# A message-passing layer on one core: the tasks beside its batches dealt anew, early products kept in DRAM, a fifth buffer of gathered rows

## The chip, the cores and the metric

The kernel runs on one core of a Trainium2 chip. The metric is the device time of one execution in microseconds (us). The core's engines run side by side, each through its own queue in order: TensorE (PE, with its weight loads PEld) multiplies matrices, VectorE (DVE) and ScalarE (ACT) work on elements, GpSimd (POOL) issues the gathers, SyncE (SP) issues other transfers. They wait for one another by semaphores.

## The reference

1250 nodes have 512 features each, 384 as 128 vectors of three and 128 scalars s. 40000 edges are sorted by their target `dst`. Two rounds of messages follow each other; cut to what matters:

```python
x_j = x[src]
s_j = silu(x_j[:, 384:] @ W1 + b1) @ W3 + b3
split = s_j * (rbf * cutoff @ W2 + b2)             # rbf, cutoff: functions of edge_weight
s1, s2, s3 = thirds of split
v_msg = v_j * s1[:, :, None] + s3[:, :, None] * edge_attr[:, None, :]
x = x + segment_sum([v_msg, s2], dst)              # first round
x_j = x[src]
... v @ U, (v @ U) @ V, norm, an MLP with Wu1, Wu2: a row of 512 for each edge
x = x + segment_sum(msg, dst)                      # second round
out = layernorm(x_in + x)
```

A row of the second round depends on the source node alone. So it is computed once for each node, and its sum over edges is a product of a 1250 x 1250 table of edge counts with the table of rows.

## The kernel before

**Head.** For each of ten blocks of 128 nodes, `table_row` makes a row of 640 for every node, and SP writes it to a table in DRAM. Between these rows stand transposings of the edges' data (`beside`).

**Batches.** The edges are cut into 20 groups of 16 tiles of 128 edges, and a batch `t` is four tiles (80 batches, the last four smaller). `gather(t)` has POOL fetch 4 x 128 rows of the table by four indirect transfers into a buffer `rows_t` (four buffers, `ROWS`). `edge_factors(t)` has PE make the factors `eb` in four PSUM banks, of which there is one set. `messages(t)` has DVE multiply rows by factors (two instructions, L799 and L802, with `make_pair`, L816, between them). `add_messages(t)` has PE sum the messages by target node with one-hot matrices (`hot`, `spread`) into `agg`. ACT's `mark_sources` and DVE's `make_pair` make matrices whose product, `count_links`, counts edges for each pair of source and target in `adj`. `close_group` has ACT copy `agg` and split the counts (`high`, `both`); DVE's `add_counts` brings them into the table of counts.

**Tasks beside the batches.** A step of the main loop emits gather(t+2), messages(t), the list `first`, add_messages(t-1) and count_links(t-1), the list `early`, edge_factors(t+1), the list `late` and the list `dve`. The lists, by step, are written out by hand; they set the order of each engine's queue. In them stand the making of the next group's basis, `hot` and `spread` (`make_turns`, `make_basis`, `turn_basis`, `make_hot`, `make_spread`), and for each block of nodes whose two groups are closed a chain from `sum_block` over `take_block`, `turn_nodes`, `times_u`, `times_uv`, `lengths`, `root`, `hidden`, `curve`, `factors`, `scale_row` and `end_row` to `part_row`, which leaves a block of the second round's rows as three bf16 parts. All of these use one PSUM bank, `work`, in turn, and ACT or DVE must copy out what PE put there before PE can use it again.

**Units.** The output block b needs, for each source block a, a unit of three matmuls (counts by the three parts). Units whose rows are ready are begun in the loop (`begin_out`): 37 of 100, for seven output blocks. Six sums are copied to SBUF tiles of their own (`begun_b`, 2048 bytes a partition each), the seventh stays in PSUM.

**Tail.** `load_x` and `load_rest` bring x and x1 (`resid`, kept in DRAM) back, POOL adds them and the begun sums, PE does the remaining 63 units between the links of the last block's chain and behind it, `end_out` and `norm_out` add, normalize and write each block.

Of the kernel before, what the change touches and what calls it, by code (L numbers as in the profile page):

```python
# [20 lines left out]
P = 128  # L21
# [14 lines left out]
CPG = 4  # L36
# [501 lines left out]
def windowed(tc, sh):  # L538
# [20 lines left out]
    ROWS = 4  # L559
# [34 lines left out]
    resid = tc.dram_tile([NP, width], F32, name="resid")  # L594
    counts = sh.counts
# [10 lines left out]
    with tc.tile_pool(name="msg", bufs=4) as pool, tc.tile_pool(  # L606
# [15 lines left out]
        quarter = pool.tile([P, 1], F32, name="quarter", bufs=1)  # L622
        fade = pool.tile([P, NE], F32, name="fade", bufs=1)
# [8 lines left out]
        def ratios():  # L632
            nc.vector.tensor_scalar(ratio, every, 1.0 / R_CUT, 1.0, op0=ALU.mult, op1=ALU.min)
            nc.vector.memset(quarter, 0.25 * TWO_PI)

# [66 lines left out]
        def make_turns(g, n, part):  # L702
# [16 lines left out]
            if part == 3 or part == 2 and g > 0:  # L719
                nc.scalar.activation(args, args, AF.Sin, scale=TWO_PI)  # L720
# [44 lines left out]

        def mark_sources(t):

            g, i = batches[t]
            one = pool.tile([P, CPG, P], F16, name="one", bufs=3)
            for j in tiles(g, i):  # L770
                e = g * EPG + i * CPG + j
                nc.scalar.activation(one[:, j, :], number[:, :P], AF.Abs, bias=low[:, e : e + 1])  # L772
            for j in tiles(g, i):
                e = g * EPG + i * CPG + j
                nc.scalar.activation(  # L775
                    one[:, j, :], one[:, j, :], AF.Relu,
                    scale=less[:, e : e + 1], bias=worth[:, e : e + 1],
                )
            onehots[t] = one
# [13 lines left out]
        def messages(t):  # L793
# [6 lines left out]
            make_pair(t)  # L800
            for js, n, m in runs(g, i):
# [64 lines left out]
        def close_group(g):  # L866
# [5 lines left out]
            else:  # L872
                if g + 2 < NGR:
                    assert rows == P
                    sums[g + 2] = pool.tile([P, width], F32, name="sums_1", bufs=2)
                    nc.scalar.copy(sums[g + 2][P - WIN :, :], agg[P - WIN :, :])
# [3 lines left out]
                rows = min(rows, KEPT)  # L880
                nc.scalar.copy(sums[g][:rows, :], agg[:rows, :])
# [7 lines left out]
            boths[g] = both  # L889

        def add_counts(g):
            both = boths.pop(g)
# [3 lines left out]
            del adjs[g]  # L896

# [19 lines left out]
        def sum_block(b):  # L917
            blk = work()
            for k in range(2):
                nc.tensor.matmul(  # L920
                    blk, sh.sel[:, k, :], sums.pop(2 * b + k), start=(k == 0), stop=(k == 1)
                )
            blks[b] = blk
# [152 lines left out]
        def load_x(first):  # L1076
# [5 lines left out]
            for b in range(first, first + n):  # L1082
                if b in (0, NB - 1):
                    load_nodes(nc.scalar, sh, to, b, b + 1, cols, first)
            inner = [b for b in range(first, first + n) if b not in (0, NB - 1)]
            load_nodes(nc.scalar, sh, to, inner[0], inner[-1] + 1, cols, first)
            for k in range(n):
                kept[first + k] = to[:, k, :]

        def load_rest(first):  # L1090
            n = min(5, NB - first)
            to = five_rows("msg", 2)
            nc.scalar.dma_start(to[:, :n, :], rows_from(resid, first, n))
# [20 lines left out]
        def begin_out(b, a, last, kept):  # L1114
            if a == 0:
                accs[b] = ps_sum.tile([P, BANK], F32, name="begun")
            products(accs[b], b, a, a + 1, a == 0, last and not kept)
# [12 lines left out]
        def end_out(b):  # L1130
# [8 lines left out]
            nc.vector.tensor_scalar(scale[:, 0:1], moments[:, 1:2], EPS, None, op0=ALU.add)  # L1139
            nc.scalar.activation(scale[:, 0:1], scale[:, 0:1], AF.Sqrt)  # L1140
            ending[b] = row, moments, scale

        def norm_out(b):
            row, moments, scale = ending.pop(b)
            nc.vector.reciprocal(scale[:, 0:1], scale[:, 0:1])
            nc.vector.tensor_scalar(
                scale[:, 1:2], moments[:, 0:1], scale[:, 0:1], -1.0, op0=ALU.mult, op1=ALU.mult
            )
# [13 lines left out]
        def at(when, step, fn, *args):  # L1162
            when.setdefault(step, []).append((fn, args))

        def pair_turns(g, part, t):
            n = min(2, NGR - g)
            if n > 0:
                at(dve, t, make_turns, g, n, part)

        for k in range(3):  # L1170
            pair_turns(1, k, 0)
        for g in range(NGR):
            at(early, last_step[g] + 1, close_group, g)
            at(dve, last_step[g] + 1, add_counts, g)
        for t, (g, i) in enumerate(batches):
            if t + 1 < NT:
                at(early, t, mark_sources, t + 1)
            if g + 1 < NGR:
                if g % 2:
                    if i == 0:  # L1180
                        at(dve, t, make_hot, g + 1)
                        at(early, t, turn_basis, g + 1)
                    elif i == 1:
                        at(dve, t, make_spread, g + 1, 0)
                        pair_turns(g + 2, 0, t)
                    elif i == 2:
                        at(dve, t, make_spread, g + 1, 1)
                else:
                    if i == 1:
                        at(dve, t, make_hot, g + 1)  # L1190
                    elif i == 2:
# [504 lines left out]
```

## Time and profile before

| | us |
|---|---|
| median of 10 runs (546.73 to 554.81) | 551.78 |
| the profiled execution | 546.12 |
| its span, first to last instruction | 544.3 |
| first gather starts | 34.12 |
| last multiply of batch 75 ends | 461.69 |
| last multiply of batch 79 ends | 481.00 |
| PE's last matmul ends | 535.37 |

The page gives busy time of each engine, the chain that ended last, and groups of instructions with mean time and with what ended the idle time in front of them. "Issue" is a gap for which the profile shows no other cause. A row of the timeline is a start, a duration, the engine, the line, output and inputs, and in brackets the idle time before it and who ended that.

### The profile page before, as it was taken

How to read it: one execution, taken by the hardware profiler on the slowest of the kernel's cores; microseconds unless marked ns; L12 is line 12 of the kernel's file. 1: busy time of each engine (PE TensorE's matmuls, PEld its weight loads, DVE VectorE, ACT ScalarE, POOL GpSimd, SP SyncE). 2: the span in 40 equal slices, each digit the busy share in tenths (PEclk: the TensorE clock that was granted, in tenths of full speed). 3: DMA queues.
4: the chain of work that ended last, by engine and by line, in shares of the span. 5: the costliest groups of instructions: out<-in, count | busy, mean ns of one | idle time of the engine just before them, and what ended most of it. 6: DMA issues, size and time to landing. Idle time of an engine off the chain costs nothing.

```text
span 544.3 us, 11102 instructions
## 1 busy us (share of the span) xinstructions
PE 439.8 (81%) x4280; PEld 235.0 (43%) x4318; DVE 429.3 (79%) x594; ACT 359.3 (66%) x897; POOL 362.1 (67%) x364
## 2 busy tenths in 40 slices
PE   3946777878878778888987888887989788999993
PEld 2522333444444344444444444544545444445441
DVE  6687988888978998697897899789789689550681
ACT  1436476695795885779579588687867958723342
POOL 7337777777777777777777777677777774100960
PEclk9976878989889988897998999999899899999998
DMA  8658888888878878888787887778787876109131
GB/s 249 212 181 240 251 250 260 258 256 257 264 234 249 267 236 248 262 253 249 245 262 229 252 259 230 233 236 252 233 247 240 250 225 187 49 5 346 50 136 61
DMA packets 35178, 121.18 MB, mean 223 GB/s; under 512 B 6365, under 2 KB 7912, under 8 KB 35116
## 3 DMA queue, kind: packets, MB, share of 16 engines
q0 software_dynamic: 26016, 104.86, 62.9%
q1 hardware_dynamic: 5124, 9.69, 4.9%
q10 hardware_dynamic: 3976, 5.82, 3.1%
q8 instruction: 36, 0.59, 0.4%
q14 instruction: 26, 0.21, 0.1%
HBM read 111.89 MB, written 8.46 MB: 221 GB/s over the span
## 4 chain that ended last, share of the span: by engine, by line
PE 30%; DVE 27%; DMA 18%; POOL 8%; issue 7%; ACT 7%; DVEq 0%; POOLq 0%; ACTq 0%
DMA rows_t<-table,src_i 12%; DVE msg L802 11%; POOL rows_t L691 7%; DVE msg L799 5%; PE agg L833 5%; PE eb L787 5%; DMA wu_sb<-in_L_gnn_Wu_dram 4%; PE agg L840 4%; PE work L981 3%; DVE pair L816 3%; PE adj L1105 2%; PE agg L1105 2%; PE eb L1105 2%; ACT one L775 2%; DVE spread L760 1%
## 5 line engine op out<-in xcount | busy, mean ns | idle before, releaser
L691 POOL DMA_INDIRECT rows_t<-table,src_i x313 | 325.6, 1040 | 118.8 <-issue 79.6
L802 DVE TENSOR_TENSOR msg<-rows_t,eb 128x1536 f32<-128x1536 f32 (+1 forms) x81 | 137.0, 1692 | 0.0
L775 ACT ACTIVATE one<-one,weight,src_f 128x128 f16<-128x128 f16 x313 | 128.1, 480 | 0.2 <-DVE magic L674 0.2
L799 DVE TENSOR_TENSOR msg<-rows_t,eb 128x1024 f32<-128x1024 f32 (+1 forms) x81 | 95.4, 1179 | 38.2 <-PE eb L787 29.3
L787 PE MATMUL eb<-w_sb,basis_t 21*128 21x384 f32 x626 | 77.1, 548 | 57.5 <-DVE msg L802 56.3
L772 ACT ACTIVATE one<-number,low 128x128 f16<-128x128 f16 x313 | 99.4, 389 | 2.5 <-DVE low L665 1.4
L833 PE MATMUL agg<-msg,hot 128*32 128x512 f32 x626 | 96.4, 673 | 0.0
L840 PEld LDWEIGHTS agg<-msg,spread 128*32 128x32 f32 x1878 | 62.5, 121 | 58.0 <-issue 57.5
L840 PE MATMUL agg<-msg,spread 128*32 128x128 f32 x1878 | 76.7, 296 | 0.0
L787 PEld LDWEIGHTS eb<-w_sb,basis_t 21*128 21x128 f32 x626 | 27.1, 187 | 82.3 <-issue 51.5
L1105 PEld LDWEIGHTS <-counts 128*128 128x128 f16 x300 | 29.1, 99 | 27.6 <-issue 2.5
L1098 POOL TENSOR_TENSOR msg<-msg,rows_t 128x512 f32<-128x512 f32 (+1 forms) x10 | 13.7, 1379 | 37.5 <-PE eb L1105 37.5
L816 DVE TENSOR_TENSOR pair<-number,column 128x640 f16<-128x640 f16 (+1 forms) x81 | 38.4, 475 | 0.0
L760 DVE TENSOR_TENSOR spread<-hot,attr 128x768 f32<-128x768 f32 x40 | 37.9, 949 | 0.0
L858 PE MATMUL adj<-pair,one 128*128 128x160 f16 x313 | 37.7, 245 | 0.0
L893 DVE SCALAR_TENSOR_TENSOR both<-both,adj 128x400 f16<-128x400 f16 (+1 forms) x20 | 11.3, 567 | 31.6 <-ACT both L888 29.1
L981 PE MATMUL work<-ident,square 128*128 128x128 f32 x60 | 14.0, 379 | 20.7 <-ACT basis_t L743 20.6
L1038 ACT COPY x<-work 128x128 f32<-128x128 f32 x10 | 2.7, 266 | 41.2 <-PE work L981 41.2
L858 PEld LDWEIGHTS <-one 128*128 128x128 f16 x313 | 21.1, 101 | 18.0 <-issue 15.2
L833 PEld LDWEIGHTS agg<-msg,hot 128*32 128x32 f32 x626 | 13.1, 111 | 33.4 <-issue 25.1
L1105 PE MATMUL begun<-store,counts 128*128 128x512 bf16 x84 | 25.1, 379 | 1.7
L743 ACT COPY basis_t<-work 128x512 f32<-128x512 f32 x20 | 11.5, 576 | 22.7 <-PE work L738 22.7
(170 smaller groups left out, 560.6 us busy)
## 6 DMA issues: line engine op xcount, KB each, us to landing
rows_t<-table,src_i POOLq DMA_INDIRECT x313, 4.1
resid<-x SPq DMA_DIRECT2D x10, 256.0 KB
msg<-resid ACTq DMA_DIRECT2D x2, 1280.0 KB
rows_t<-in_x_dram ACTq DMA_DIRECT2D x2, 1024.0 KB
out_dram<-msg SPq DMA_DIRECT2D x8, 256.0 KB
table<-msg SPq DMA_DIRECT2D x6, 320.0 KB
store<-in_x_dram POOLq DMA_DIRECT2D x2, 768.0 KB
table<-rows_t SPq DMA_DIRECT2D x4, 320.0 KB
```

The costliest lines, as they stand in the source:

```text
L691: nc.gpsimd.indirect_dma_start(out=rows_t[:n, j, :], out_offset=None, in_=sh.table1, in_offset=bass.IndirectOffsetOnAxis(ap=sh.src_i[:n, g ...
L760: nc.vector.tensor_mul(spread[g][:, at], hots[g][:, at, None, :].to_broadcast([P, n, 3, WIN]), sh.attr[:, g, at, :, None].to_broadcast([P, ...
L772: nc.scalar.activation(one[:, j, :], number[:, :P], AF.Abs, bias=low[:, e : e + 1])
L775: nc.scalar.activation(one[:, j, :], one[:, j, :], AF.Relu, scale=less[:, e : e + 1], bias=worth[:, e : e + 1],)
L787: nc.tensor.matmul(eb[:, j, :V], turned[g][rows, i, :], sh.w2_sb[rows, :], start=True, stop=True,)
L799: nc.vector.tensor_mul(msg[:m, js, V:], rows_t[:m, js, V:], eb[:m, js, C:V])
L802: nc.vector.tensor_mul(msg[:m, js, :V].rearrange("p t (k c) -> p t k c", k=3), rows_t[:m, js, :V].rearrange("p t (k c) -> p t k c", k=3), ...
L816: nc.vector.tensor_tensor(pair[:m, js, :].rearrange("p t (l h) -> p t l h", h=2), number[:m, : PARTS * WIN].rearrange("p (l h) -> p l h", ...
L833: nc.tensor.matmul(agg[j * WIN : (j + 1) * WIN, :], hots[g][:m, i * CPG + j, :], msg[:m, j, :width], start=(i == 0), stop=False, skip_grou ...
L840: nc.tensor.matmul(agg[j * WIN : (j + 1) * WIN, c * C : (c + 1) * C], spread[g][:m, i * CPG + j, c, :], msg[:m, j, width:], start=False, s ...
L858: nc.tensor.matmul(to[:, :, at : at + WIN], one[:m, j, :], pair[:m, j, :].rearrange("e (p n) -> e p n", n=WIN), start=(i == 0 and j == js[ ...
L1105: nc.tensor.matmul(acc, counts[:, a, b * P : (b + 1) * P], table2(a, k), start=(start and a == first and k == 0), stop=(stop and a == end ...
```

## The change

- `ROWS` is 5: a fifth buffer of gathered rows (10240 bytes a partition).
- Begun sums are copied to one tile `begun` and written to DRAM (`spilled`) by SP; `load_begun` brings them back into two gather buffers in the tail. All eight begun blocks go this way. The slots of units are dealt over the steps: 40 units are begun.
- The lists are sorted by a rank within a step. The tasks of two groups and of a block are dealt over eight steps. `add_counts` is parted into `low_counts` and `keep_counts`, some steps apart; `mark_sources` into `distances` (list `first`) and the rest (`early`); `sum_block` into its two matmuls. `make_pair` follows both multiplies. The last block's chain takes seven steps in place of eight.
- In the head only two tasks stand between the table's rows; the others follow behind them, and the first group's `spread` follows batch 0's messages.
- The loads of the tail move from ACT's queue to SP's. Of the end of a block, two small instructions move from DVE to ACT.

```diff
-    ROWS = 4
+    ROWS = 5
...
+    spilled = tc.dram_tile([NP, width], F32, name="spilled")
...
             for js, n, m in runs(g, i):
                 nc.vector.tensor_mul(msg[:m, js, V:], rows_t[:m, js, V:], eb[:m, js, C:V])
-            make_pair(t)
-            for js, n, m in runs(g, i):
                 nc.vector.tensor_mul(
...
-        def add_counts(g):
-            both = boths.pop(g)
+            if g % 2 and g + 2 < NGR:
+                assert rows == P
+                sums[g + 2] = pool.tile([P, width], F32, name="sums_1", bufs=2)
+                nc.scalar.copy(sums[g + 2][P - WIN :, :], agg[P - WIN :, :])
+
+        def low_counts(g):
+            both = boths[g]
             nc.vector.scalar_tensor_tensor(
                 both[:, 0], both[:, 1], -PACK, links(g), op0=ALU.mult, op1=ALU.add
             )
             del adjs[g]
+
+        def keep_counts(g):
+            both = boths.pop(g)
...
+        def load_begun(first):
+            n = min(5, len(begun) - first)
+            to = five_rows("rows_t", ROWS)
+            nc.sync.dma_start(to[:, :n, :], rows_from(spilled, first, n))
+            for k in range(n):
+                partial[first + k] = to[:, k, :]
...
-            if last and not kept:
-                partial[b] = pool.tile([P, width], F32, name=f"begun_{b}", bufs=1)
-                nc.scalar.copy(partial[b], accs.pop(b))
+            products(accs[b], b, a, a + 1, a == 0, last)
+            if last:
+                to = pool.tile([P, width], F32, name="begun", bufs=1)
+                nc.scalar.copy(to, accs.pop(b))
+                nc.sync.dma_start(spilled[b * P : (b + 1) * P, :], to)
...
-            nc.vector.tensor_scalar(scale[:, 0:1], moments[:, 1:2], EPS, None, op0=ALU.add)
-            nc.scalar.activation(scale[:, 0:1], scale[:, 0:1], AF.Sqrt)
-            ending[b] = row, moments, scale
+            nc.scalar.activation(scale[:, 0:1], moments[:, 1:2], AF.Sqrt, bias=eps)
+            nc.scalar.activation(scale[:, 1:2], moments[:, 0:1], AF.Identity, scale=-1.0)
+            ending[b] = row, scale
...
+            at(early, end, 0, close_group, g)
+            at(dve, end, 5, low_counts, g)
+            at(dve, end + (2 if g % 2 else 3), 3, keep_counts, g)
...
+                at(early, base + 5, 1, turn_basis, g + 1)
...
+        slots = ((7, late), (6, early), (0, early), (1, late), (3, late), (5, late), (2, late), (4, late))
+        for c, of in zip(range(4, NB), ((0,), (1, 2), (3, 4), (5,), (6,), (7,))):
...
         for first_b in range(0, NB, 5):
-            at(dve, free, load_x, first_b)
-            at(dve, free + 1 if first_b + 5 < NB else ends[NB - 1] - 5, load_rest, first_b)
+            at(dve, NT - 2, 8, load_x, first_b)
+            at(dve, NT, 8, load_begun, first_b)
+            at(dve, free + 1, 8, load_rest, first_b)
...
-            beside = {
-                0: (turn_weights, number_sources), 2: (turn_sources, ratios),
-                4: (lambda: turn_attr(0), lambda: make_turns(0, 1, 0)),
-                5: (lambda: turn_attr(1), lambda: make_turns(0, 1, 1)),
-                6: (lambda: turn_attr(2), lambda: make_turns(0, 1, 2)),
-            }
+            beside = {0: number_sources, 2: turn_sources}
```

Three places show how the order of instructions moved. First DVE where a group of edges is closed beside block 3's chain (x_2310 is that block's row of nodes): before, between two batches,

```order
L799 TENSOR_TENSOR msg<-rows_t,eb 128x4x256
L816 TENSOR_TENSOR pair<-number,column 128x640
L802 TENSOR_TENSOR msg<-rows_t,eb 128x4x384
L893 SCALAR_TENSOR_TENSOR both<-both,adj 128x400
L899 COPY counts<-both 128x2x5x64
L904 TENSOR_TENSOR counts<-counts,both 128x2x5x16
L747 TENSOR_TENSOR hot<-lane,local 128x512
L1048 TENSOR_TENSOR x_2310<-x_2310,store 128x512
L799 TENSOR_TENSOR msg<-rows_t,eb 128x4x256
```

and the same place of the changed kernel:

```order
L807 TENSOR_TENSOR msg<-rows_t,eb 128x4x256
L808 TENSOR_TENSOR msg<-rows_t,eb 128x4x384
L822 TENSOR_TENSOR pair<-number,column 128x640
L763 TENSOR_TENSOR spread<-hot,attr 128x768
L899 SCALAR_TENSOR_TENSOR both<-both,adj 128x400
L807 TENSOR_TENSOR msg<-rows_t,eb 128x4x256
L808 TENSOR_TENSOR msg<-rows_t,eb 128x4x384
L822 TENSOR_TENSOR pair<-number,column 128x640
```

The instruction that reads `both` (L893, now L899) has moved behind a `spread`, and the two that follow it have left for a later batch; the pair stands behind both multiplies. Second ACT at the copy that empties `work` after a basis was transposed (`basis_t`), before:

```order
L871 COPY sums_2944<-agg 128x512
L886 ACTIVATE high<-adj,magic 128x400
L888 ACTIVATE both<-high,magic 128x400
L772 ACTIVATE one<-number,low 128x128 x4
L775 ACTIVATE one<-one,weight,src_f 128x128 x4
L743 COPY basis_t<-work 128x512
L992 ACT_TABLE_LOAD
L992 ACTIVATE n_t<-work 128x128
```

and after the change, from the same copy of sums on:

```order
L877 COPY sums_2948<-agg 128x512
L888 ACTIVATE high<-adj,magic 128x400
L890 ACTIVATE both<-high,magic 128x400
L968 COPY vu<-work 128x384
L785 ACTIVATE one<-one,weight,src_f 128x128 x4
L979 ACTIVATE square<-work 128x384
L981 COPY vv<-work 128x384
L775 ACTIVATE one<-number,low 128x128 x4
L746 COPY basis_t<-work 128x512
L785 ACTIVATE one<-one,weight,src_f 128x128 x4
```

`basis_t` now stands a batch behind the closing of the group and between the two halves of `one`, and `vu`, `square` and `vv` follow the closing. Third DVE in the head, before:

```order
L633 TENSOR_SCALAR ratio<-weight 128x320
L634 MEMSET quarter 128x1
L530 TENSOR_TENSOR rows_t<-store,pp 128x384
L530 TENSOR_TENSOR msg<-store,pp 128x384
L708 TENSOR_TENSOR turn<-ratio,half_n 128x320
L530 TENSOR_TENSOR msg<-store,pp 128x384
L714 TENSOR_SCALAR whole<-turn 128x320
L530 TENSOR_TENSOR msg<-store,pp 128x384
L718 TENSOR_TENSOR turn<-turn,whole 128x320
L530 TENSOR_TENSOR msg<-store,pp 128x384 x3
L641 RECIPROCAL vv<-weight 128x320
```

and after the change:

```order
L530 TENSOR_TENSOR rows_t<-store,pp 128x384
L530 TENSOR_TENSOR msg<-store,pp 128x384 x6
L635 TENSOR_SCALAR ratio<-weight 128x320
L636 MEMSET quarter 128x1
L637 MEMSET eps 128x1
L711 TENSOR_TENSOR turn<-ratio,half_n 128x320
L717 TENSOR_SCALAR whole<-turn 128x320
L721 TENSOR_TENSOR turn<-turn,whole 128x320
L644 RECIPROCAL vv<-weight 128x320
```

The rows of the table (L530) now follow each other without the work that stood between them.

More of the change, by code (lines that the diff above doesn't have):

```diff
@@ L1160, in windowed @@
         first, early, late, dve = {}, {}, {}, {}
[L1162 to L1171, printed above, removed]
-        for g in range(NGR):
-            at(early, last_step[g] + 1, close_group, g)
-            at(dve, last_step[g] + 1, add_counts, g)
-        for t, (g, i) in enumerate(batches):
-            if t + 1 < NT:
[L1177 to L1191, printed above, removed]
-                        at(dve, t, make_basis, g + 1)
-                        at(dve, t, make_spread, g + 1, 0)
-                    elif i == 3:
-                        at(first, t, turn_basis, g + 1)
-                        at(dve, t, make_spread, g + 1, 1)
-                        if g + 2 < NGR:
-                            at(dve, t, make_basis, g + 2)
@@ L1315, in windowed @@
         edge_factors(0)
-        for t in range(max(*early, *late, *dve) + 1):
+        for t in range(max(*first, *early, *late, *dve) + 1):
             if t + ahead < NT:
```

175 lines of the change are left out of this document (109 added, 66 removed).

## The prediction

> **What bounds the kernel now.** I read the page first, then the engines by stage, then GpSimd's (POOL's) own rows, then what VectorE (DVE) and TensorE (PE) wait for in the late batches, and last the head and the tail.
>
> ```profile
> PE 439.8 (81%) x4280; PEld 235.0 (43%) x4318; DVE 429.3 (79%) x594; ACT 359.3 (66%) x897; POOL 362.1 (67%) x364
> L691 POOL DMA_INDIRECT rows_t<-table,src_i x313 | 325.6, 1040 | 118.8 <-issue 79.6
> ```
>
> No engine is full, and PE at 81% is not PE at its peak. The gathers decide more than their 67% says: 325.6 us of gathering comes with 79.6 us of "issue", the gap behind each gather, so POOL is taken for 405 of 544.3 us. The stages differ:
>
> ```profile
> core 0: us, PE busy (x) PEld busy (x) DVE busy (x) ACT busy (x) POOL busy (x), PEclk, DMA share, GB/s
> 34.00:97.00 63.00, 43.56 (x448) 20.26 (x452) 54.09 (x69) 39.11 (x106) 48.40 (x48) 0.76 0.80 243
> 97.00:225.60 128.60, 103.68 (x1157) 57.64 (x1153) 109.83 (x134) 94.35 (x241) 99.36 (x96) 0.92 0.81 252
> 225.60:442.00 216.40, 181.49 (x2012) 99.60 (x2030) 187.53 (x228) 167.86 (x426) 164.34 (x157) 0.95 0.79 244
> ```
>
> The second row holds 96 gathers, 24 batches: 128.6 / 24 = 5.36 us a batch. There POOL waits for no buffer:
>
> ```profile
> L691 POOL DMA_INDIRECT rows_t<-table,src_i x96 | 99.4, 1035 | 29.3 <-issue 25.0 <-DMA rows_t<-table,src_i 1.5 <-DVE msg L799 0.9
> 45.30 0.95 POOL L691 DMA_INDIRECT rows_t<-table,src_i  x1 [0.30 <-issue]
> ...
> 92.14 0.95 POOL L691 DMA_INDIRECT rows_t<-table,src_i  x1 [0.30 <-DVE pair L816]
> ...
> 97.15 1.26 POOL L691 DMA_INDIRECT rows_t<-table,src_i  x1 [0.30 <-issue]
> 98.72 0.95 POOL L691 DMA_INDIRECT rows_t<-table,src_i  x1 [0.30 <-issue]
> ...
> 225.77 0.95 POOL L691 DMA_INDIRECT rows_t<-table,src_i  x1 [0.30 <-DVE turn L718]
> ```
>
> The first row groups those 96; 97.15 and 225.77 start the first of them and the one behind the last. Undisturbed, a gather takes 0.95 and its gap 0.30, so four take 5.00; the 0.36 above that is gathers like the 1.26. So POOL's own pace with all the block work beside it is 5.36 a batch, 42.9 per eight. Late in the loop the kernel is slower than that, and there DVE sets the pace:
>
> ```profile
> 304.14 1.75 DVE L802 TENSOR_TENSOR msg<-rows_t,eb 128x1536 f32<-128x1536 f32 x1
> 349.30 1.75 DVE L802 TENSOR_TENSOR msg<-rows_t,eb 128x1536 f32<-128x1536 f32 x1
> L799 DVE TENSOR_TENSOR msg<-rows_t,eb 128x1024 f32<-128x1024 f32 x8 | 9.7, 1214 | 3.2 <-PE eb L787 3.2
> L893 DVE SCALAR_TENSOR_TENSOR both<-both,adj 128x400 f16<-128x400 f16 x2 | 1.1, 572 | 3.2 <-ACT both L888 2.3 <-PE begun L1105 0.9
> POOL rows_t L691 <- DVE msg L802: 6.2, 6, 1.6
> DVE both L893 <- ACT both L888: 11.5, 7, 2.3
> PE work L981 <- ACT basis_t L743: 10.5, 4, 2.8
> ```
>
> The first two rows are eight batches apart: 45.16 us, 5.64 a batch. Of these DVE idles 6.4 (the two grouped rows for just those eight), so its work is 38.8, or 4.84 a batch. POOL, faster by itself, now waits for buffers (the last three rows, of waits, cover 262 to 441 us). Two orders make DVE's idle time. It asks for `both` (L893) before ACT has written it. And PE stands behind ACT's queue:
>
> ```profile
> 291.53 1.31 PE L981 MATMUL work<-ident,square 128*128 128x128 f32 x6 [2.79 <-ACT basis_t L743]
> 297.94 1.22 DVE L799 TENSOR_TENSOR msg<-rows_t,eb 128x1024 f32<-128x1024 f32 x1 [2.39 <-PE eb L787]
> ```
>
> PE lost 2.79 us at L981 since the one `work` bank was still to be emptied by a copy behind `close_group` and four pairs of `one` on ACT; the next factors `eb` were late, and DVE stood 2.39.
>
> **The change, part by part.**
>
> *Dealing anew (loop).* DVE's instructions stay, 4.84 us a batch. `low_counts` and `keep_counts` are parted, two to three steps apart; the copies that free `work` stand ahead of `mark_sources` on ACT; `make_pair` follows both multiplies, so `eb`'s banks come free one pair sooner (some 0.5, its row stands further down), and what is left of the 4.84 beside the two multiplies (1.21 and 1.75), some 1.9 a batch, covers `eb`. PE's busy time per batch is 181.49 x 5.36 / 216.4 = 4.5 and ACT's 4.2, both below 5.36. So I expect DVE's 6.4 to shrink below the 42.9 - 38.8 = 4.1 from which POOL sets the pace throughout. What is late next is then the gather itself. For the lead of a gather over its multiplies in such a state I take a batch early in the loop:
>
> ```profile
> 55.71 0.95 POOL L691 DMA_INDIRECT rows_t<-table,src_i  x1 [0.30 <-issue]
> 65.31 1.75 DVE L802 TENSOR_TENSOR msg<-rows_t,eb 128x1536 f32<-128x1536 f32 x1
> 459.95 1.74 DVE L802 TENSOR_TENSOR msg<-rows_t,eb 128x1536 f32<-128x1536 f32 x1
> 480.05 0.95 DVE L802 TENSOR_TENSOR msg<-rows_t,eb 128x768 f32<-128x768 f32 x1
> 34.12 1.05 POOL L691 DMA_INDIRECT rows_t<-table,src_i  x1 [13.87 <-DVE fade L644]
> ```
>
> From batch 4's first gather to the end of its multiplies: 67.06 - 55.71 = 11.35. Batch 75 ends at 461.69 now, 427.6 after the first gather (34.12). Then: 75 x 5.36 + 11.35 = 413.4. Gain 14.2. The pace is a mean of a stretch with the same work; its ends are 5.20 (45.30 to 92.14 above, nine batches with little block work) and 5.45, a tenth over it if the denser work blocks more gathers: 12.0 more, 6.8 less.
>
> *Batches 76 to 79* (461.69 to 481.00) hold nine gathers in place of sixteen, and PE is all but full around them. I take them unchanged: 0.
>
> ```profile
> 442.00:481.00 39.00, 37.32 (x347) 18.98 (x354) 28.38 (x44) 25.74 (x63) 13.96 (x14) 1.00 0.42 126
> ```
>
> *Fifth buffer.* It lets POOL run one batch further ahead, 5 us, when DVE stalls. Where POOL sets the pace the buffers stand empty, so by itself it is worth 0; it is cover for the first part. It can cost nothing on POOL's queue, which holds no new instruction there.
>
> *Spilled units.* Eight copies on ACT as before in kind (six before), eight 256 KB writes on SP's queue, and in the tail two loads. In the loop SP has only the `resid` writes. In the tail SP's in-order queue now carries x, the last spill, two loads of spills, `resid` and its two loads; the loads of x can start before the last batches end, since their buffers come free with batches 75 and 76. The additions on POOL wait for all of them:
>
> ```profile
> 503.81 1.48 POOL L1098 TENSOR_TENSOR msg<-msg,rows_t 128x512 f32<-128x512 f32 x1 [37.47 <-PE eb L1105]
> 512.16 0.69 DVE L1133 TENSOR_TENSOR msg<-msg,agg 128x512 f32<-128x512 f32 x1 [0.52 <-PE agg L1105]
> ```
>
> The first of them is 22.8 after the last multiply. Eighteen additions of about 1.3 (sixteen now) are 23.4, and the first block is ended (second row) 31 after it. I price it 0; if the loads come as late as now, the two more additions cost up to 2.6.
>
> *Tail on PE.* Forty units (node block by source block, three matmuls) are begun in the loop, thirty-seven before, so 60 remain in place of 63.
>
> ```profile
> 522.26 6.64 PE L1105 MATMUL agg<-store,counts 128*128 128x512 bf16 x30
> 528.73 6.64 PE L1105 MATMUL adj<-store,counts 128*128 128x512 bf16 x29
> 535.48 0.69 DVE L1133 TENSOR_TENSOR msg<-msg,adj 128x512 f32<-128x512 f32 x1 [4.40 <-PE adj L1105]
> ```
>
> Thirty matmuls take 6.47, so a unit 0.65; DVE waits 4.40 for PE at the end, so PE is the path and three units gain 1.9. The last block's chain, started earlier, is covered by units either way; the two small DVE instructions per end that go to ACT are off the path: 0. In the loop three units cost 1.9 over 48 batches, inside PE's slack.
>
> *Head.* The table's rows:
>
> ```profile
> 17.72 0.67 DVE L530 TENSOR_TENSOR rows_t<-store,pp 128x384 f32<-128x384 f32 x1 [2.28 <-DMA w_sb<-in_L_gnn_b_dram]
> 18.95 0.68 DVE L530 TENSOR_TENSOR rows_t<-store,pp 128x384 f32<-128x384 f32 x1
> 20.16 0.67 DVE L530 TENSOR_TENSOR rows_t<-store,pp 128x384 f32<-128x384 f32 x1 [0.54 <-ACT rows_t L529]
> ...
> 30.16 0.68 DVE L530 TENSOR_TENSOR msg<-store,pp 128x384 f32<-128x384 f32 x1 [0.53 <-ACT msg L529]
> ```
>
> Undisturbed, rows come 1.21 apart; nine of these are 10.9, and now it takes 12.44, so the work between rows costs 1.55. Of its five transposings one stays: gain 4/5, 1.2. The gather follows the last row by its write's landing (30.84 to 34.12), so the loop starts 1.2 sooner. The work moved behind it runs on DVE beside the first four gathers; two `spread` go behind batch 0.
>
> *Sum*: 14.2 + 1.9 + 1.2 = 17.3, less 1.3 for DVE's lag at the loop's end (one stall half the size of the 2.39): 16.0. The profiled execution took 546.12 (span 544.3), so 530.1. The median of the ten runs shown is 551.78, 5.7 above it; I take the same 16.0 off that: 535.8. Less than 0.5% (2.8 us) can't be told from no change here.
>
> **A rule that speaks against it.** A gather that starts while DVE runs an instruction with two inputs in SBUF is stretched to about that instruction's end:
>
> ```profile
> 283.63 1.54 POOL L691 DMA_INDIRECT rows_t<-table,src_i  x1 [0.30 <-issue]
> 283.69 0.70 DVE L729 TENSOR_TENSOR basis<-turn,fade 128x320 f32<-128x320 f32 x1
> 280.85 1.23 POOL L691 DMA_INDIRECT rows_t<-table,src_i  x1 [0.30 <-issue]
> 280.75 0.50 DVE L816 TENSOR_TENSOR pair<-number,column 128x640 f16<-128x640 f16 x1
> ```
>
> Both gathers pass 0.95 by 0.28 and 0.59, and both end some 0.8 after DVE's instruction did. The Trainium skill ("SBUF — State Buffer", section "Who interferes with whom") says that a VectorE instruction with two SBUF inputs and a GpSimd instruction that reads SBUF exclude each other, the later one blocking fully. The trace agrees.
>
> **The rivals.**
>
> *Port (slower).* DVE's tasks now stand in one unbroken row behind every batch, about 1.9 us long, against a gather's start each 1.25. In step with POOL, the same one or two starts could be hit each time. For it: the two stretched gathers above. Against: the total of such instructions is unchanged, and in the POOL-paced stretch they cost 0.36 a batch. From 0.36 + 17.3 / 75 = 0.59 a batch on the gain is gone; two starts hit for 0.35 each, 0.70, give 75 x 0.34 = 25.5 more, or 561.
>
> *Other waits take their place.* `turn_basis` (PE) now asks for a basis that DVE makes last in the step before; ACT gets `close_group`, `vu`, `square` and `vv` in one step; and PE drops to half clock where it idles (0.76 between 34 and 97, where data comes last). If DVE still idles 6.4 in eight batches the loop gains nothing beyond its head: 551.8 - 3.1 = 548.7. Against it: PE and ACT fit, and five buffers carry a stall over. The Trainium skill ("TensorE: Matmul & The Clock Gate", section "HAM oscillation — how this bites in real kernels") warns that a loop which waits for transfers lets PE's clock fall again and again. The row of 34 to 97 agrees.
>
> *Nothing from the buffer.* If POOL paces, four or five buffers make no difference; that is within the forecast, not beside it.
>
> **How the numbers follow.** POOL-paced loop: 0.72, 535.8, its own range 524 (pace 5.20) to 543 (5.45). Other waits: 0.15, up to 548.7, most of it still over 0.5% faster. Port: 0.07, 561. The rest, 0.06, is spread, half of it faster. The range takes the forecast's lower end and reaches into the second case: 524 to 548. Faster 0.72 + 0.12 + 0.03 = 0.87; same 0.03 + 0.02 = 0.05; slower 0.07 + 0.01 = 0.08.
>
> **What would show it.** Right: POOL's rows with no wait for DVE's multiplies, about 5.36 a batch from first to last; DVE's longest wait is for the gather's DMA; L981 no longer waits near 2.8 for `basis_t`; first gather near 32.9; last multiply near 466. Wrong: POOL still waiting for L808, or gathers with a mean over 1.10 us (above 1.035), or POOL's additions in the tail holding the ends of blocks.

## The result, and the profile after

The changed kernel takes 528.39 us (median of 18 runs, 524.06 to 532.32), the kernel before 551.18 (62 runs beside it). The ratio of their times is 0.961, 95% interval 0.959 to 0.963: 21.5 us less, 20.3 to 22.6. (Ratio and interval compare the fast runs alone, so they differ a little from the two medians, which lie 22.8 apart.) The forecast was 535.8, 16.0 less. The profiled execution took 527.59, with a span of 525.7, against 544.3 before: 18.6 less.

The page after: engines, the chain that ended last (the row below it is the chain of before), and the two groups that carry the loop.

```profile
PE 438.8 (83%) x4285; PEld 231.3 (44%) x4318; DVE 426.1 (81%) x575; ACT 367.2 (70%) x919; POOL 358.0 (68%) x366
POOL 27%; DMA 27%; PE 22%; issue 13%; DVE 8%; ACT 1%; DVEq 0%; POOLq 0%; ACTq 0%
PE 30%; DVE 27%; DMA 18%; POOL 8%; issue 7%; ACT 7%; DVEq 0%; POOLq 0%; ACTq 0%
L694 POOL DMA_INDIRECT rows_t<-table,src_i x313 | 318.7, 1018 | 106.9 <-issue 83.8
L807 DVE TENSOR_TENSOR msg<-rows_t,eb 128x1024 f32<-128x1024 f32 (+1 forms) x81 | 95.8, 1183 | 45.8 <-DMA rows_t<-table,src_i 23.6
```

DVE's longest wait is now for the gathers' data, 23.6 us, and POOL and its transfers lead the chain, where PE and DVE did. The waits that the prediction named, first before and then after (groups, and rows of the waits):

```profile
L981 PE MATMUL work<-ident,square 128*128 128x128 f32 x60 | 14.0, 379 | 20.7 <-ACT basis_t L743 20.6
L893 DVE SCALAR_TENSOR_TENSOR both<-both,adj 128x400 f16<-128x400 f16 (+1 forms) x20 | 11.3, 567 | 31.6 <-ACT both L888 29.1 <-PE eb L787 1.6 <-PE begun L1105 0.9
DVE msg L799 <- PE eb L787: 29.3, 13, 4.4
POOL rows_t L691 <- DVE msg L802: 12.6, 9, 2.3
```

```profile
L989 PE MATMUL work<-ident,square 128*128 128x128 f32 x60 | 13.2, 359 | 0.0
L899 DVE SCALAR_TENSOR_TENSOR both<-both,adj 128x400 f16<-128x400 f16 (+1 forms) x20 | 11.2, 562 | 2.7 <-ACT both L890 1.6 <-PE eb L795 1.1
DVE msg L807 <- PE eb L795: 12.2, 7, 4.4
L741 PE MATMUL work<-ident,basis 128*128 128x128 f32 x80 | 13.4, 294 | 7.0 <-DVE basis L732 6.8
```

PE's 20.6 us for `basis_t` are gone, so are DVE's 29.1 for `both`, and POOL waits for no multiply beyond its ordinary gap of 0.30 (the largest such row that is left is 2.4 us in eight gaps). `turn_basis` waits 6.8 us for its basis on PE, as the second rival feared, but no gather is held up by it.

Where the 18.6 us of span went is read from a few rows of the timeline, of after first, then the one of before that the prediction did not show.

```profile
32.43 1.05 POOL L694 DMA_INDIRECT rows_t<-table,src_i  x1 [11.84 <-DMA table<-msg]
429.63 0.95 POOL L694 DMA_INDIRECT rows_t<-table,src_i  x1 [0.30 <-DMA rows_t<-table,src_i]
440.74 1.75 DVE L808 TENSOR_TENSOR msg<-rows_t,eb 128x1536 f32<-128x1536 f32 x1
461.44 0.95 DVE L808 TENSOR_TENSOR msg<-rows_t,eb 128x768 f32<-128x768 f32 x1
```

```profile
441.94 1.03 POOL L691 DMA_INDIRECT rows_t<-table,src_i  x1 [0.30 <-DVE square L1030]
```

The rows at 429.63 (after) and 441.94 (before) are batch 75's first gather, 440.74 is batch 75's second multiply, 461.44 the last one of batch 79.

| stretch | before | after | less |
|---|---|---|---|
| up to the first gather | 34.12 | 32.43 | 1.69 |
| first gather to batch 75's first gather | 407.82 | 397.20 | 10.62 |
| from there to the end of batch 75's multiplies | 19.75 | 12.86 | 6.89 |
| batches 76 to 79 | 19.31 | 19.90 | -0.59 |
| behind the last multiply | 63.30 | 63.31 | -0.01 |

The pace of the gathers is 397.20 / 75 = 5.30 us a batch; before it was 5.44. POOL's own rows for that stretch (its length, then POOL's busy time), before, after, and of e9, a run that is told further down, say what the 10.62 us are:

```profile
34.12:441.94 407.82, 312.04 (x300) 0.91 0.80 246
32.43:429.63 397.20, 305.78 (x300) 0.92 0.83 258
34.39:438.23 403.84, 312.42 (x301) 0.92 0.82 249
```

POOL's idle time fell from 95.78 to 91.42, by 4.36. That is all that POOL had waited for multiplies (6.2 us in six places late in the loop, less six ordinary gaps of 0.30). The other 6.26 us are shorter gathers, which the forecast did not hold. The 6.89 of the third line are backlog: DVE no longer falls behind the gathers. So up to the end of batch 75's multiplies 11.25 us came as the forecast has it and 6.26 by another way, which e10 is about.

### The profile page after: what moved, and what is told of

Same layout as the page of the kernel before. It is cut to its first block, busy times and chain, and to the rows that moved or that the text cites. A ratio compares the mean times of both kernels' runs of the same rounds, so it can differ in the third digit from the quotient of the medians.

```text
span 525.7 us, 11190 instructions
## 1 busy us (share of the span) xinstructions
PE 438.8 (83%) x4285; PEld 231.3 (44%) x4318; DVE 426.1 (81%) x575; ACT 367.2 (70%) x919; POOL 358.0 (68%) x366
## 4 chain that ended last, share of the span: by engine, by line
POOL 27%; DMA 27%; PE 22%; issue 13%; DVE 8%; ACT 1%; DVEq 0%; POOLq 0%; ACTq 0%
POOL rows_t L694 26%; DMA rows_t<-table,src_i 21%; DMA bu_sb<-in_L_gnn_bu_dram 4%; DVE msg L807 4%; PE agg L839 3%; PE begun L1120 3%; DVE msg L808 3%; PE eb L795 2%; PE adj L1120 2%; PE agg L846 2%; PE eb L1120 2%; PE work L989 2%; DMA store<-in_x_dram 1%; PE work L1120 1%; DMA w_sb<-in_L_gnn_b_dram 1%
## 5 line engine op out<-in xcount | busy, mean ns | idle before, releaser
L694 POOL DMA_INDIRECT rows_t<-table,src_i x313 | 318.7, 1018 | 106.9 <-issue 83.8
L807 DVE TENSOR_TENSOR msg<-rows_t,eb 128x1024 f32<-128x1024 f32 (+1 forms) x81 | 95.8, 1183 | 45.8 <-DMA rows_t<-table,src_i 23.6
L795 PE MATMUL eb<-w_sb,basis_t 21*128 21x384 f32 x626 | 78.2, 556 | 53.7 <-DVE msg L808 52.6
L846 PE MATMUL agg<-msg,spread 128*32 128x128 f32 x1878 | 75.2, 292 | 0.0
L1120 PE MATMUL begun<-store,counts 128*128 128x512 bf16 x110 | 32.3, 391 | 3.1 <-issue 2.4
L839 PEld LDWEIGHTS agg<-msg,hot 128*32 128x32 f32 x626 | 13.1, 111 | 33.1 <-issue 22.9
L723 ACT ACTIVATE turn<-turn 128x640 f32<-128x640 f32 (+1 forms) x11 | 7.6, 689 | 20.7 <-DVE turn L721 20.7
L929 PE MATMUL work<-sums,sel 128*128 128x512 f32 x40 | 19.8, 617 | 0.0
L741 PE MATMUL work<-ident,basis 128*128 128x128 f32 x80 | 13.4, 294 | 7.0 <-DVE basis L732 6.8
```

The costliest lines, as they stand in the source:

```text
L694: nc.gpsimd.indirect_dma_start(out=rows_t[:n, j, :], out_offset=None, in_=sh.table1, in_offset=bass.IndirectOffsetOnAxis(ap=sh.src_i[:n, g ...
L795: nc.tensor.matmul(eb[:, j, :V], turned[g][rows, i, :], sh.w2_sb[rows, :], start=True, stop=True,)
L807: nc.vector.tensor_mul(msg[:m, js, V:], rows_t[:m, js, V:], eb[:m, js, C:V])
L839: nc.tensor.matmul(agg[j * WIN : (j + 1) * WIN, :], hots[g][:m, i * CPG + j, :], msg[:m, j, :width], start=(i == 0), stop=False, skip_grou ...
L846: nc.tensor.matmul(agg[j * WIN : (j + 1) * WIN, c * C : (c + 1) * C], spread[g][:m, i * CPG + j, c, :], msg[:m, j, width:], start=False, s ...
L1120: nc.tensor.matmul(acc, counts[:, a, b * P : (b + 1) * P], table2(a, k), start=(start and a == first and k == 0), stop=(stop and a == end ...
```

## The experiments

**Who sets the pace (e1, e2, e3).** An instruction that nobody needs is put on POOL or on DVE, once a batch:

```diff
+        probe = pool.tile([P, 192], F32, name="probe", bufs=1)
...
+            nc.gpsimd.memset(probe, 0.0)
             rows_of[t] = rows_t
```

> The changed kernel with one more instruction on POOL for each batch, behind its four gathers: a memset of 128 x 192 (0.26 us in the head of the changed kernel) to a tile that nobody reads. Theory A (POOL sets the pace of the changed loop from first to last): nothing hides it, so 75 batches times 0.26 to 0.31 (the memset and a small gap) is +20 to +23 us, about 550. Theory B (DVE or its waits still set the pace in the late half, POOL has 0.3 us a batch to spare there, as it had before): at most half of it, +10 us or less.

> The changed kernel with one more instruction on DVE for each batch, behind its two multiplies: a memset of 128 x 256 (estimated 0.27 us from the 0.48 us of a 16 x 512 memset) to a tile that nobody reads. Theory A (POOL paces): DVE's 4.84 us a batch become 5.1, still under POOL's 5.30, so 0 to +4 us. Theory B (DVE paces): 75 times 0.27 is +20 us.

> The kernel before with the same memset of 128 x 256 on DVE for each batch. Theory A (before, DVE with its two waits sets the pace late in the loop and POOL early): some 40 late batches times 0.27 is +9 to +13 us, clearly more than the same memset costs the changed kernel. Theory B (POOL paced the kernel before too): 0 to +4 us.

Measured: e1 539.24 (10.9 over the changed kernel), ratio to the kernel before 0.978 (0.973 to 0.983). e2 533.20 (4.8 over), 0.969 (0.962 to 0.977). e3, on the kernel before, 553.27 against 551.38 beside it: 1.006 (1.001 to 1.010), 3.1 us by the ratio (0.7 to 5.6).

The timeline of POOL in e1, and the groups of e1, e2 and e3 for the added memset and the gathers:

```profile
298.70 1.37 POOL L695 DMA_INDIRECT rows_t<-table,src_i  x1 [0.30 <-issue]
300.07 0.28 POOL L703 MEMSET probe<- 128x192 f32 x1
300.51 0.96 POOL L695 DMA_INDIRECT rows_t<-table,src_i  x1 [0.17 <-issue]
301.78 0.95 POOL L695 DMA_INDIRECT rows_t<-table,src_i  x1 [0.30 <-issue]
```

```profile
L703 POOL MEMSET probe<- 128x192 f32 x80 | 22.2, 278 | 0.0
L815 DVE MEMSET probe<- 128x256 f32 x80 | 21.8, 272 | 0.2
L695 POOL DMA_INDIRECT rows_t<-table,src_i x313 | 323.5, 1034 | 105.8 <-issue 82.0 <-DMA table<-msg 10.7 <-DMA rows_t<-table,src_i 8.5
DVE msg L800 <- PE eb L788: 25.2, 12, 4.1
DVE both L895 <- ACT both L890: 24.6, 18, 4.0
```

In e1 the memset starts at once behind a gather and the gap behind it is 0.17 in place of 0.30. So its price is 0.28 + 0.17 - 0.30 = 0.15 us, and 75 of that are 11: all of it arrives in the time. Theory A had the mechanism and the wrong price. The time alone would not tell it from theory B's 10; that the pace rose in both halves does, since B had POOL with time to spare in the late half. (Batches 0, 40 and 75 start their gathers at 32.43, 244.21 and 429.63 in the changed kernel and at 33.00, 251.72 and 442.45 in e1: 5.29 us a batch became 5.47, and 5.30 became 5.45.) In e2 the memset is 0.272 us, but it overlaps its neighbours, and DVE's busy time on the page rises by 16.0 us (426.1 to 442.1). Of these 4.8 arrive; the gathers' sum rose by as much (318.7 to 323.5, the third row), which may be chance: e4, without the memset, has 322.8. DVE does not set the pace of the changed kernel, POOL does. In e3 DVE's busy time rises by 17.0 (429.3 to 446.3); theory A expected 9 to 13 us and 3.1 came, which is theory B's number. Its reason, that POOL paced the kernel before too, goes as far as POOL's rows above: POOL waited 4.36 us for multiplies, but at batch 75 DVE was 19.75 behind its gathers. DVE's two waits were 58.4 us before and are 49.8 here (the last two rows), so 8.6 of the added work went into waits. DVE's work alone did not set the pace late in the loop before; that its waits did is what e9 tests.

**The order without the rest (e4).**

```diff
-    ROWS = 5
+    ROWS = 4
...
+                if b < 5:
+                    partial[b] = to
+                    return
                 nc.sync.dma_start(spilled[b * P : (b + 1) * P, :], to)
```

and the head of the kernel before.

> The changed kernel with the order of the tasks kept, but four buffers of gathered rows in place of five, five of the eight begun sums kept in SBUF in place of DRAM (three still written), and the head as before. Theory A (the order alone makes the gain in the loop; the fifth buffer is never needed): only the head's 1.7 us come back, time 529 to 532. Theory B (the fifth buffer carries stalls over): with four buffers POOL waits for DVE's multiplies and 5 us or more come back, 534 or more.

Measured: 531.34, 0.961 (0.955 to 0.968), 2.9 us over the changed kernel by medians, as theory A had it. POOL's group (of an execution of 535.40, the longest of the four):

```profile
L694 POOL DMA_INDIRECT rows_t<-table,src_i x313 | 322.8, 1031 | 109.0 <-issue 85.3 <-DVE fade L647 13.9 <-DMA rows_t<-table,src_i 6.4
```

With four buffers POOL still waits for no multiply, and its idle time from the first gather to batch 75's is 91.4 us, as in the changed kernel. So the fifth buffer is worth nothing to this loop, nor does the way over DRAM cost anything that shows.

**Three orders alone (e9).** The kernel before with the pair behind both multiplies, `turn_basis` of every second group first in its step, and `add_counts` parted; buffers, units, chain of a block, head and tail as before.

```diff
-            make_pair(t)
...
-                        at(early, t, turn_basis, g + 1)
+                        early.setdefault(t, []).insert(0, (turn_basis, (g + 1,)))
...
-            at(dve, last_step[g] + 1, add_counts, g)
+            at(dve, last_step[g] + 1, low_counts, g)
+            at(dve, last_step[g] + (3 if g % 2 else 4), keep_counts, g)
```

> The kernel before with three changes together: pair behind the multiplies, add_counts parted, turn_basis first in its step; four buffers, units, head and tail as before. It is the run e8 once more, whose chip ran every kernel some 28% slower (the kernel before 704 us). Theory A (the three orders make DVE's waits, and without them POOL paces from first to last): the loop's whole gain is there, 14 to 18 us under the kernel before (533 to 537). Theory B: less than 5 us, since the spread of units and chains over eight steps makes the gain. Between the two, 5 to 14 us: the three orders are a part, and the waits left over in the trace say what the rest is.

Measured: 537.74 against 549.88 beside it, 0.979 (0.969 to 0.989): 11.6 us less, 6.3 to 16.9. It lies between the theories; the interval reaches theory A's 14, not theory B's 5. Groups and waits of e9:

```profile
L691 POOL DMA_INDIRECT rows_t<-table,src_i x313 | 326.9, 1044 | 108.0 <-issue 82.3 <-DVE fade L644 12.2 <-DMA rows_t<-table,src_i 7.3
DVE both L891 <- ACT both L886: 33.1, 18, 4.0
DVE msg L799 <- PE eb L787: 12.5, 10, 4.9
438.23 0.95 POOL L691 DMA_INDIRECT rows_t<-table,src_i  x1 [0.30 <-issue]
451.98 1.74 DVE L800 TENSOR_TENSOR msg<-rows_t,eb 128x1536 f32<-128x1536 f32 x1
34.39 1.05 POOL L691 DMA_INDIRECT rows_t<-table,src_i  x1 [12.21 <-DVE fade L644]
```

The wait for `eb` fell from 29.3 to 12.5 us and POOL no longer waits for multiplies. The wait for `both` did not fall, 33.1: `close_group` had moved back on ACT behind `basis_t`. It stands there and holds up no gather. So of the three, the parting of `add_counts` did not do what it was for. What each of the three is worth, e5 to e7 were to say and can't.

From the first gather (34.39) to batch 75's (438.23) e9 takes 403.84, 5.38 a batch; the changed kernel takes 397.20. Of that 6.64 the gathers themselves explain all: POOL's busy time is 312.42 here and 305.78 there (the rows under the table), and its idle time is 91.42 in both. Against the kernel before, e9 has all of the 4.36 of idle time and none of the shorter gathers. The other differences: 1.96 by the head, 2.63 by the end of batch 75's multiplies (15.49 behind its first gather, 12.86 there); whether the wait for `both` makes these, no run shows.

**The long gathers (e10).** The changed kernel with pairs for the first two batches only, and `hot`, `spread`, turns and basis for the first two groups only, used again. (The sums of later groups lack their own edges' data.)

```diff
+            if t > 1:
+                pairs[t] = kept_pairs[t % 2]
+                return
...
         def make_spread(g, half):
+            if g > 1:
+                spread[g] = spread[g % 2]
+                return
```

> The changed kernel without most of DVE's instructions that read two inputs from SBUF: the pairs are made for the first two batches only and hot, spread, turns and basis for the first two groups only, and used again (so the edges' data of later groups are left out of the sums). The multiplies of the messages, PE, ACT and the gathers stay as they are. Theory A (the 0.3 us a batch by which POOL's pace stands over its undisturbed 5.00 come from gathers that start during such an instruction on DVE): the gathers' mean falls from 1018 to about 955 ns, the pace from 5.30 to 5.0 to 5.1, and the time by 15 to 22 us, to 506 to 513. Theory B (the long gathers are POOL's or the DMA rings' own): mean and pace stay, and with DVE off the path already the time falls by less than 4 us.

Measured: 511.95, 0.930 (0.925 to 0.936), 16.4 us under the changed kernel. First a stretched gather of the changed kernel with DVE beside it, then e10:

```profile
202.69 1.72 POOL L694 DMA_INDIRECT rows_t<-table,src_i  x1 [0.30 <-issue]
202.63 0.95 DVE L763 TENSOR_TENSOR spread<-hot,attr 128x768 f32<-128x768 f32 x1
```

```profile
202.58 0.95 POOL L694 DMA_INDIRECT rows_t<-table,src_i  x1 [0.30 <-issue]
200.44 1.75 DVE L818 TENSOR_TENSOR msg<-rows_t,eb 128x1536 f32<-128x1536 f32 x1
L694 POOL DMA_INDIRECT rows_t<-table,src_i x313 | 300.8, 961 | 107.3 <-issue 86.2 <-DMA table<-msg 12.2 <-DVE msg L817 4.6
```

The changed kernel's gather starts 0.06 behind the start of a `spread` and ends at 204.41, 0.83 behind its end. Without those instructions a gather is 0.95 (mean 961 ns), although DVE still multiplies rows by factors from PSUM 2.9 us in each batch. Theory A holds: over 313 gathers of 0.95 the stretches add 318.7 - 297.4 = 21.3 us in the changed kernel, 29.5 in e9, 28.2 before, 3.4 here. That DVE has less to do in e10 is no rival, since POOL's rows show the time gone from the gathers themselves. The Trainium skill ("SBUF — State Buffer", section "Who interferes with whom") says that a DVE instruction with at most one SBUF input, outside the modes that use both ports, does not contend with GpSimd. For the multiplies this run agrees: their one SBUF input is `rows_t`. A copy with one SBUF input, `counts<-both`, does stretch a gather here:

```profile
177.12 0.32 DVE L921 COPY counts<-both 128x640 f16<-128x640 f16 x1
177.18 1.07 POOL L694 DMA_INDIRECT rows_t<-table,src_i  x1 [0.30 <-issue]
```

Which mode that copy ran in, the trace does not show.

**More units in the loop (e11, e12).**

```diff
-        for c, of in zip(range(4, NB), ((0,), (1, 2), (3, 4), (5,), (6,), (7,))):
+        for c, of in zip(range(4, NB), ((), (0,), (1, 2), (3, 4), (5, 6), (7, 8))):
```

> The changed kernel with 52 units begun in the loop in place of 40 (blocks 0; 1, 2; 3, 4; 5, 6; 7, 8 in the windows of five to nine closed blocks), so 48 left for the tail. Theory A (PE has room under POOL's pace: it waits 52.6 us in all for DVE's multiplies): the tail is 12 x 0.65 = 7.8 us shorter, the loop at most 3 us longer, time 521 to 525. Theory B (two units a step make PE, some 4.7 us busy a batch now, the bound from batch 64 on): eb comes late, what the tail gains the loop loses, within 2 us of the changed kernel.

Measured: 527.15, 0.958 (0.952 to 0.963), 1.2 us under the changed kernel by medians and not to be told from it. Busy times by stretch, of the changed kernel (batches 76 to 79, the rest up to PE's last matmul) and of e11 (the same batches, the rest of the span), each with the weight loads for units beside batches 76 to 79, three a unit:

```profile
core 0: us, PE busy (x) PEld busy (x) DVE busy (x) ACT busy (x) POOL busy (x), PEclk, DMA share, GB/s
442.49:462.39 19.90, 19.27 (x145) 9.36 (x147) 11.68 (x21) 12.53 (x28) 3.52 (x4) 1.00 0.63 208
462.39:516.32 53.93, 51.97 (x264) 27.10 (x265) 23.07 (x52) 23.48 (x55) 23.72 (x18) 1.00 0.39 137
L1120 PEld LDWEIGHTS <-counts 128*128 128x128 f16 x12 | 1.1, 103 | 1.0 <-issue 0.5
```

```profile
core 0: us, PE busy (x), PEclk, DMA share, GB/s
443.80:467.12 23.32, 22.02 (x174) 1.00 0.61 190
467.12:525.00 57.88, 45.01 (x233) 0.95 0.41 142
L1120 PEld LDWEIGHTS <-counts 128*128 128x128 f16 x21 | 2.0, 101 | 2.9 <-issue 1.5
```

Behind the last multiply e11 takes 525.1 - 467.12 = 58.0 in place of 63.3, but batches 76 to 79 take 23.32 in place of 19.90. The time is theory B's, but the pace is not: the loop up to batch 75 did bear two units a step (batch 75's gathers start at 431.47, the first at 33.07: a pace of 5.31). PE is all but full from batch 75's end on (19.27 of 19.90, 51.97 of 53.93), so a unit put beside those batches is paid there. Three of the 12 added units stand there (21 weight loads in place of 12), by 0.65 a unit some 1.9 of the 3.4 us; the rest is not traced. The run that puts all extra units ahead of batch 76 was e12.

**Five runs that tell nothing.** While they ran, the kernel before took 703 to 704 us. e5, e6 and e7 are the three parts of e9 alone, e8 is e9 itself, e12 has 44 units, none beside batches 76 to 79.

> The kernel before with one thing changed: the pair is made behind both multiplies in place of between them. Theory A (DVE's waits for eb and for both made the late batches slow, each of the named moves takes away a part of them): the four PSUM banks of eb come free 0.5 us earlier, DVE's wait for eb (29.3 us in all) shrinks by a half or more, and the time falls by 3 to 7 us. Theory B (the gain comes from the units and the chain of a block being spread over eight steps, not from this order): within 2 us of the kernel before.

> The kernel before with one thing changed: add_counts is parted, its first instruction stands last among DVE's tasks of the step in which the group is closed, the other two follow 2 or 3 steps later. Theory A: DVE's wait for both (29.1 us in all) all but goes; half of it comes back as a wait for eb or the gather, so the time falls by 3 to 8 us. Theory B: within 2 us of the kernel before.

> The kernel before with one thing changed: turn_basis of every second group stands first in its step, so that ACT empties the work bank before it closes the group and makes the four pairs of one. Theory A: PE's wait of 2.8 us for basis_t at the transposing of squares goes, DVE's wait for eb shrinks by about 2 us in eight batches (nine times), and the time falls by 3 to 8 us. Theory B: within 2 us of the kernel before.

> The kernel before with the three changes of the other runs together (pair behind the multiplies, add_counts parted, turn_basis first in its step); four buffers, units, head and tail as before. Theory A: POOL paces from first to last, and the loop's whole gain is there, 14 to 18 us (533 to 537). Theory B: less than 5 us, since the spread of units and chains makes the gain.

> The changed kernel with 44 units begun, all of them before batch 76 (blocks 0; 1, 2; 3, 4; 5, 6 in the windows of six to eight closed blocks, as in e11, then 7 units of block 7 within four steps), none beside batches 76 to 79, and 56 left for the tail. Theory A (behind batch 75 PE is full to its last matmul, so only a unit that is done under POOL's pace is saved; the changed kernel has some 36 units before batch 76, this one 44): 8 x 0.65 = 5.2 us less, and up to 1.5 us back for a later end of batch 75, so 523 to 525; batches 76 to 79 take 17 to 18 us in place of 19.9. Theory B (the tail is set by the latency of the last block's chain, not by PE's work): the units taken away beside batches 76 to 79 save time there, but the tail stays at 63 us, so 526 to 528.

Measured: 703.88, 694.97, 705.66 and 710.76 beside 704.08 for the kernel before; e12 717.17 beside 702.70. e8 came out slower than the kernel before and e9, the same kernel, faster, so these five say nothing of the kernels at 551. What a single one of the three orders is worth, and whether e12 beats the changed kernel, stays open.

## Why the prediction was right, point by point

- **POOL paces from first to last: right.** e1 and e2 show it. The pace of 5.36 came out as 5.30, 4.8 us in 75 batches. The pace was taken from a stretch with the same DVE work, as if only the amount counted; where DVE's instructions stand against the gathers' starts counts too (28.2 us of stretches before, 21.3 after, 29.5 in e9 with nearly the same work). By the rows, gathers that end some 0.8 us behind a `pair` made 7.5 us of the stretches before and 2.0 after, but 7.2 in e2, where a memset stands ahead of the pair. Nothing in the change was meant to shorten gathers, and e4, in nearly the same order, has stretches of 25.4 (322.8 - 297.4). So these 4.8 us were luck, as far as the runs show.
- **"There DVE sets the pace" (before, late): right only with DVE's waits counted in.** The 45.16 us for eight batches were right. DVE's work alone did not hold the loop: e3 added 17.0 us to it and 3.1 came. What held it were waits that went round PE, ACT and DVE: e9 took the one for `eb` from 29.3 to 12.5 and POOL's for multiplies away, with nearly the same work on DVE. POOL itself waited just 4.36 us up to batch 75; the larger part was DVE's backlog (19.75, now 12.86).
- **DVE's 6.4 us of idle time had to shrink under 4.1: not needed in that form.** The half of it for `both` shrank in the changed kernel (29.1 to 1.6) and stayed in e9 (33.1), where POOL paces too. In this loop idle time counts only when POOL runs out of buffers over it.
- **Lead and lag (11.35 and 1.3): right in size.** From batch 75's first gather to its last multiply's end are 12.86, 1.5 more than 11.35. The reason given, one stall at the loop's end, is not shown: over the batches 0 to 75 of the changed kernel the same stretch lies anywhere between 10.8 and 13.0.
- **Fifth buffer 0, spills 0: right so far as e4 tells,** within an interval of some 7 us. POOL's additions start 17.2 us behind the last multiply (479.57; before 22.8), earlier than priced, and hold nothing.
- **Head 1.2: 1.69.**
- **Tail 1.9: nothing came.** Three units fewer should be 1.9 on PE. The weight loads for units (three a unit) from batch 75's end to the last matmul, before and after, show only two units fewer there, so 1.3:

```profile
L1105 PEld LDWEIGHTS <-counts 128*128 128x128 f16 x201 | 19.7, 98 | 23.3 <-issue 2.5
L1120 PEld LDWEIGHTS <-counts 128*128 128x128 f16 x195 | 19.1, 99 | 21.6 <-issue 1.7
```

  From batch 75's end to the last matmul PE was busy 72.13 us before and 71.24 after, 0.9 less, and idle 1.0 more. Before, from the windows:

```profile
461.69:481.00 19.31, 19.21 (x146) 9.16 (x147) 11.12 (x22) 10.86 (x24) 2.89 (x3) 1.00 0.13 40
481.00:535.37 54.37, 52.92 (x257) 26.77 (x259) 25.36 (x66) 19.49 (x36) 21.25 (x16) 1.00 0.39 140
```

  The idle time is in this row of the changed kernel, block 8's last link, which stood ahead of the last batch's sums before and now stands behind the block sum whose bank DVE must empty first:

```profile
469.28 0.29 PE L1018 MATMUL work<-bias,ones_r 33*128 33x128 f32 x1 [1.04 <-DVE x L941]
```

  So of the 1.9, one unit (0.65) had not moved ahead of batch 76, the new wait took what the other two gave, and the remaining 0.4 us is not found; some matmul records may be missing.
- **Batches 76 to 79 taken as unchanged: 0.6 more.**
- **The port rival did not come,** since the stretches fell by 6.9 us; but e10 shows that its mechanism is real and is the next thing that the loop pays for: 16.4 us. Of its two examples one does not fit the words: the gather at 283.63 starts 0.06 us ahead of the `basis` at 283.69 and is stretched all the same. So the trace agrees that the two exclude each other, not that the one that is recorded later waits.
- **The sum.** 16.0 were forecast and 18.6 came in the profiled executions: pace +4.8, head +0.5, lag -0.2, batches 76 to 79 -0.6, tail -1.9. So the total is nearer than its parts: of the 12.9 that the loop's waits were to give (14.2 less 1.3) 11.25 came, the tail gave nothing, and shorter gathers, unforeseen, made up for both. The runs differ by more, 21.5, because the profiled execution of before was 5.1 us under its median and that of after 0.8. The step "I take the same 16.0 off that" assumed that the slower executions lose the same; which part of a median execution of before is longer, no trace here shows.

## What to carry to other kernels

First name the engine that could pace the loop undisturbed, here POOL with 5.0 us a batch, and ask of every wait whether it makes that engine wait; 33 us of waits that do not (e9, `both`) held up no gather. Test a claimed bound by adding an instruction to that engine: what arrives in the time is the answer (11 of 11 us on POOL, 4.8 of 16 on DVE). Work moved out of a full tail should be a gain only where it lands under the pace of another engine; e11 points to that, but no run here shows it.

## What was not expected of the hardware

- The gap of 0.30 us behind each gather is no dead time: a memset of 0.28 on POOL started with no gap behind a gather, the gap behind it was 0.17, and it cost 0.15.
- A gather that starts in a DVE instruction with two SBUF inputs, or just ahead of it, ends about 0.8 us behind that instruction, so that one `spread` made it 1.72 in place of 0.95; with such instructions all but gone, the 313 gathers took 17.9 us less in all.
